# Output tiles at the seam of two attention stages, bias additions in other units, and the last two tiles stored apart

## The chip, the cores and the metric

The kernel runs on one core of a Trainium2 chip. Every time is a device time in microseconds (us) of one execution. Engines are named as the profile names them: PE is TensorE's matmuls and PEld its weight loads, DVE is VectorE, ACT is ScalarE, POOL is GpSimd, SP is SyncE, which here only issues DMAs.

## The reference, cut to what matters

One transformer block on two batches of 1024 rows of 256 columns, all float32. `x_attn` attends to itself and then to a context of 154 rows of 192; both have 16 heads of 64.

```
h = layernorm(x, ln1_g, ln1_b)
x = attention(h, h, sa_wq, sa_wk, sa_wv) @ sa_wo + sa_bo + x
h = layernorm(x, ln2_g, ln2_b)
x = attention(h, cond, ca_wq, ca_wk, ca_wv) @ ca_wo + ca_bo + x
h = layernorm(x, ln3_g, ln3_b)
p = h @ ff_w1 + ff_b1                      # 2 x 1024 columns: a, gate
x = (a * gelu(gate)) @ ff_w2 + ff_b2 + x
```

A bias such as `sa_bo` is one row of 256 that is added to every row of x. It can be added to x at any time after layernorm has read x for this attention and before the next layernorm reads it.

## The kernel before, in words

x stays in SBUF, in tiles of 128 rows (`xt`). For each batch there are 8 of them. The whole program is written as one fixed order of slots: `tc.manual_schedule()` means that each engine gets its instructions in the order in which the Python code issues them. Each engine works through its own queue in that order and waits on semaphores where data or a buffer isn't ready.

**Self attention, 128 slots `p` (16 units of 8).** A unit is a batch and a pair of heads; units 0 to 7 are batch 0, units 8 to 15 batch 1. In one slot, PE computes two groups of 64 query rows' scores (`s`, L381, eight matmuls each; the profile counts each float32 matmul as two). DVE takes their row maxima (`st`, L541). ACT takes the exponentials (`p`, L392), with the sums beside. Halves of the rows' statistics lie on other partitions, so SP exchanges them with four small DMAs (`st<-st`, L402). One slot later POOL joins them (`dd` L410 to L412, then `ee` on ACT L414, then `zz`, `den` L416 and L418), DVE takes reciprocals (`rd`, L488), and POOL scales the exponentials (`p`, L492). Two slots later DVE transposes them (`pT`, L506). The other half of a slot's PE time is either a quarter of a head pair's weighted values (`po`, L428), in four slots out of eight, or pieces from lists: `run_work` takes from `work` (projections of the next unit: `pq`, `pk`, `pv`), from `side` (pieces of a layernorm) and from `outs` (output tiles). Without `full`, a slot takes one such piece, with it two:

```
full = hg % 2 == 0 or outs or p >= SA - 2 * SH
run_work(2 if full else 1, 1, sum_tile)
```

The score tiles come from a PSUM pool of two, so the scores of a slot wait until the exponentials of the slot before are taken. Projections and output tiles share another PSUM pool of two (`mm`), which is freed by ACT's copies or DVE's additions.

**Output tiles (`out_piece`, L354).** Four matmuls (`py`) multiply half of the heads' results for 128 rows with `wo`, and DVE adds the result to x in the next slot (L366). Batch 1's first half of heads is complete after unit 11. Its 8 tiles are `("sa", 1, 0, t)`: tiles 0 to 3 go into units 12 and 13, two a unit, tiles 4 to 7 into unit 15.

**Bias additions (`add_biases`, L255).** They put one addition for each of the 8 tiles on `later`. A self attention slot takes one function from `later`, a context attention slot up to two. The addition is POOL's (L261). For batch 0's self attention they are queued before the first slot, behind weight loads; for others `norm_beside` queues them at the end of the layernorm's pieces. After the last addition of batch 1, the next stage's bias is loaded by SP into the same tile.

**Context attention, 48 slots `c`, three a unit,** and then the feed forward, 64 slots `k`. Slot `c` = 0 follows slot `p` = 127 directly; the last slots' transposes, joins and weighted values of self attention run out beside the slots `c` = 0 to 4 (`self_drain`, `self_values`). The scores there are `sc` (L653), their maxima `neg` (L658), and the projections `pq_ca`, `pk_ca`, `pv_ca`. The place where self attention ends and context attention begins is called the seam. The feed forward ends with `sum_slot`, whose `store` (L847) adds two tiles' sums to x and stores both with one DMA.

Of the kernel before, what the change touches and what calls it, by code (L numbers as in the profile page):

```python
# [10 lines left out]
ALU = mybir.AluOpType  # L11
AX = mybir.AxisListType

P = 128
# [4 lines left out]
def tile_transformer_block(ctx: ExitStack, tc: tile.TileContext, a: dict, out: bass.AP):  # L19
    nc = tc.nc  # L20
# [10 lines left out]
    NT = S // P  # L31
# [235 lines left out]
    def norm_beside(kind, b):  # L267

        after = {"sa": None, "ca": "sa", "ff": "ca"}[kind]
        stats, deviation, normalize, turn = norm_pieces(kind, b)
        n = 1 if narrow(kind, b) else 2
        lag = {}
        for fns, first in ((turn, 3), (stats, 0), (deviation, 1), (normalize, 2)):
            for i, fn in enumerate(fns):
                t = i if fns is stats else 2 * i + 1
                lag.setdefault(first + t // n, []).append((fn, fns is turn))
        for k in range(NT // n + 3):  # L280
            tiles = range(k * n, min((k + 1) * n, NT))
            needs = [(after, b, half, t) for half in range(2) for t in tiles if after]

            def step(fns=lag[k]):
                done = [fn() for fn, _ in fns]
                return next((fn for fn in done if fn), None)

            side.append((any(turns for _, turns in lag[k]), needs, step))
        side.append((False, (), lambda: add_biases(kind, b)))


    def project_half(dst, name, wt, h, n, mul=None, parts=1):
# [261 lines left out]
    def self_beside(ui):  # L554

        if ui + 2 >= NU:
            load_pair("ca", ui + 2 - NU)
        elif ui > 0:
            load_pair("sa", units[ui + 2][1])
        nxt = self_pieces(*units[ui + 1]) if ui + 1 < NU else cross_pieces(*units[0])  # L560
        if ui + 1 < NU:
            work.extend(nxt)
        else:

            spare["out"] = mm_tile
            last = [lambda t=t: out_piece("sa", B - 1, 0, t) for t in range(NT // 2, NT)]
            work.extend(nxt[:2] + last[:2])
            held.extend(nxt[2:] + last[2:])
        if HP <= ui < NU - 2:
            ob, oh = divmod((ui - HP) // HP, 2)  # L570
            t0 = (ui % HP) * 2
            out_pieces("sa", ob, oh, (t0, t0 + 1))
        if ui == 1:
            norm_beside("sa", 1)
        if ui == NPAIR + HP:
            norm_beside("ca", 0)

# [254 lines left out]
    def sum_slot():  # L832

        k = gated.pop(0)
        blk, f = divmod(k, NF)
        b, t0 = divmod(blk * TF, NT)
        if f == 0:
            sums[blk] = [sum_tile(f"pf{blk}_{i}") for i in range(TF)]
        for i in range(TF):
            nc.tensor.matmul(  # L840
                sums[blk][i][:, :D], lhsT=sums[blk, "u"][:, f, i * P:(i + 1) * P], rhs=w2[:, f, :],
                start=(f == 0), stop=(f == NF - 1),
            )
        if f < NF - 1:
            return None

        def store():  # L847
            for i in range(TF):
                t = t0 + i
                xs = xt[b, t // GT][:, t % GT, :]  # L850
                nc.vector.tensor_tensor(xs, sums[blk][i][:, :D], xs, ALU.add)
            t = t0 % GT
            nc.sync.dma_start(
                out=out[b, t0 * P:(t0 + TF) * P, :].rearrange("(t p) d -> p t d", p=P),
                in_=xt[b, t0 // GT][:, t:t + TF, :],
            )

        return store


    with tc.manual_schedule():
        stats, deviation, normalize, turn = norm_pieces("sa", 0, True)
        q0, q1, k0, k1, *values = self_pieces(*units[0])
        spare["bank"] = sum_tile

        def emit(*pieces):
            for piece in pieces:
                run(piece)
            flush(stores)


        warm = mm_tile("warm")

        def busy(n):
            for _ in range(n):
                nc.tensor.transpose(warm[:, :P], ident, ident)

        busy(32)
        emit(stats[0], stats[1], deviation[0])
        emit(stats[2], normalize[0], stats[3], deviation[1])  # L880
        copies = turn[0]()
        busy(10)
        emit(stats[4], normalize[1])
        copies()
        emit(stats[5], deviation[2])
        copies = turn[1]()
        busy(4)
        copies()
        emit(normalize[2], stats[6], stats[7], deviation[3])
        q_copy, copies = q0(), turn[2]()  # L890
        emit(normalize[3])
        q_copy()
        copies()
        k_copy, copies = k0(), turn[3]()
        k_copy()
        copies()
        emit(k1)
        later.append(lambda: load_pair("sa", units[1][1]))
        later.append(lambda: load_pair("sa", units[2][1]))
        later.extend(lambda t=t: load_x(nc.scalar, B - 1, t) for t in range(0, NT, 2))  # L900
        later.append(lambda: load_out("sa", nc.scalar))
        side.append((True, (), turn_rows))
        side.extend((True, (), lambda b=b: turn_context(b)) for b in range(B))
        work.extend([q1] + values)
        add_biases("sa", 0)

        for p in range(SA):
            if p % (2 * SH) == 0:
                self_beside(p // (2 * SH))
            if p == SA - SH:  # L910
                work.extend(held)
                held.clear()
            then = self_first(p)
            flush(stores)
            late = then()
            if p >= LAG:
                turn_groups(p - LAG)
            flush(adds)
            if late:
                late()  # L920
            if later:
                later.pop(0)()
            h, hg = divmod(p, SH)
            if h == 0 or hg < LAG:

                full = hg % 2 == 0 or outs or p >= SA - 2 * SH
                run_work(2 if full else 1, 1, sum_tile)
            else:
                run(lambda: self_values(h - 1, hg - LAG))

        for c in range(CA):
            if c == 0:
                pTc["ring"] = pt_.tile(
                    [P, 2 * NK, QH // 2], F32, tag="pT", name="pT_ca"
                ).rearrange("p a b -> p (a b)")[:, :3 * 2 * NB * NT * KB].rearrange(
                    "p (u n j q) -> p u n j q", u=3, n=NB, j=2)
            if c == SH + 1:
                out_pieces("sa", B - 1, 1, range(NT))
                outs.append(lambda: load_out("ca"))
            if c == SH + 1:  # L940
                w1, w2 = hold_gated()
            if c % len(CG) == 0:
                cross_beside(c // len(CG))
            if c % len(CG) == len(CG) - 1:
                work.extend(held)
                held.clear()
            flush(adds)
            then = cross_first(c)
            flush(stores)
            flush(lates)  # L950
            lates.append(then())
            if c <= SH:
                self_drain(SA + c)
            cross_regroup(c)
            cross_drain(c)
            cross_weigh(c)
            flush(stores)
            run_work(2, 1, n_sum=2 * (SH < c < 2 * NPAIR and c % len(CG) == 0))
            if SH - LAG < c <= SH:
                run(lambda: self_values(2 * NU - 1, c - SH + LAG - 1))  # L960
            for _ in range(min(2, len(later))):
                later.pop(0)()

        for k in range(FF):
            c = CA + k
            flush(adds)
            gate_slot(k)
            flush(stores)
            flush(lates)
            if k == 3 * len(CG):  # L970
                norm_beside("ff", B - 1)
            cross_regroup(c)
            cross_drain(c)
            cross_weigh(c)
            flush(stores)
            if k == 0:
                out_pieces("ca", B - 1, 0, range(NT - 2 * TF, NT))
            if k == len(CG) + 2:
                out_pieces("ca", B - 1, 1, range(NT))
            if k > len(CG) + 2:  # L980
                for _ in range(min(2, len(gated) - 1)):
                    run(sum_slot)
                flush(stores)
            run_work(2, 1)
            if later:
                later.pop(0)()
        while gated:
            run(sum_slot)
            flush(stores)
# [32 lines left out]
```

## Time and profile before

| | us |
|---|---|
| runs of the kernel before, three | 1166.22, 1167.21, 1169.26; median 1167.21 |
| profiled execution | 1166.33 |
| its span, first to last instruction | 1164.5 |
| PE busy in the span | 1141.3 (98%) |
| DVE, ACT, POOL busy | 828.9, 643.3, 665.8 |
| POOL bias addition, one (L261) | 0.73 |
| DVE addition of an output tile (L366) | 0.41 |
| matmuls of one output tile, eight records in the trace | 1.8 |
| mean granted TensorE clock | 0.997 |

A clock of 1 is TensorE's full speed. A line of the profile names the line of the kernel (L261), the tile that is written and the tiles that are read (`x<-x,sa_bo`), and, in brackets, how long the engine had been idle and what released it.

### The profile page before, as it was taken

To read this page: it belongs to the slowest core of one execution; us is meant where nothing else is said; L and a number is where in the kernel's file an instruction comes from. 1 tells how busy PE (TensorE), PEld (TensorE's weight loads), DVE (VectorE), ACT (ScalarE), POOL (GpSimd) and SP (SyncE) were. 2 spreads that over 40 slices of the span, in tenths; PEclk is the share of its full clock that TensorE was granted. 3 is DMA by queue.
4 is the path that set the end of the run, shared out by engine and by line. 5 is a ranking of instruction groups with operands and counts; after the bars stand their busy time and mean duration, and the time that the engine had idled before them with its cause. 6 is when DMAs were issued, how large, how long until landed. Compare 5 with 4: busy or idle time off the path is not lost.

```text
span 1164.5 us, 31710 instructions
## 1 busy us (share of the span) xinstructions
PE 1141.3 (98%) x11931; PEld 673.2 (58%) x11931; DVE 828.9 (71%) x1170; ACT 643.3 (55%) x2055; POOL 665.8 (57%) x1556
## 2 busy tenths in 40 slices
PE   8999999999999999999999999899999999999998
PEld 5434444545545545545545455565566567888887
DVE  4888998898889889888999899557555664232222
ACT  5666676666666656656666666538655572041111
POOL 1778777876777777677777788626644453030000
PEclk9999999999999999999999999899999999999999
DMA  2311011111101101101111010167444433000000
GB/s 80 98 41 34 12 26 34 21 21 34 21 16 35 21 17 26 26 19 21 25 26 21 18 29 11 42 159 183 115 104 99 99 82 69 7 13 10 19 10 18
DMA packets 87234, 51.21 MB, mean 44 GB/s; under 512 B 30814, under 2 KB 77866, under 8 KB 87082
## 3 DMA queue, kind: packets, MB, share of 16 engines
q1 hardware_dynamic: 83866, 46.57, 17.5%
q10 hardware_dynamic: 3216, 2.62, 0.7%
q8 instruction: 94, 1.54, 0.6%
q14 instruction: 58, 0.48, 0.1%
HBM read 19.52 MB, written 2.10 MB: 19 GB/s over the span
## 4 chain that ended last, share of the span: by engine, by line
PE 82%; ACT 6%; POOL 3%; DVE 3%; DMA 2%; issue 2%; SPq 1%; DVEq 0%; ACTq 0%; POOLq 0%
PE po L428 16%; PE s L381 16%; PE pa L817 10%; PE py_sa L359 5%; PE py_ca L359 5%; PE pq_ca L298 5%; PE pf L840 5%; PE poc L729 4%; ACT p L392 4%; PE pv_sa L314 4%; PE pk_sa L298 3%; PE sc L653 3%; PE pq_sa L298 3%; DMA st<-st 2%; DVE st L541 2%
## 5 line engine op out<-in xcount | busy, mean ns | idle before, releaser
L392 ACT ACTIVATE p<-s,st 128x512 f32<-128x512 f32 x512 | 344.7, 685 | 217.9 <-DVE st L541 206.3
L492 POOL TENSOR_SCALAR p<-p,rd,ee 128x512 f32<-128x512 f32 x512 | 385.6, 767 | 43.7 <-DVE rd L488 42.7
L541 DVE TENSOR_REDUCE st<-s 128x2 f32<-128x1024 f32 x256 | 301.2, 1218 | 43.1 <-PE s L381 34.7
L506 DVE STREAM_TRANSPOSE pT<-p 128x1024 f32<-128x1024 f32 x256 | 302.3, 1218 | 1.7 <-POOL p L492 1.7
L381 PE MATMUL s<-k_sa,q_sa 64*32 64x512 f32 x4096 | 253.4, 596 | 12.5 <-ACT p L392 11.2
L428 PE MATMUL po<-pT,v_sa 64*64 64x256 f32 x4096 | 235.8, 379 | 0.0
L428 PEld LDWEIGHTS po<-pT,v_sa 64*64 64x64 f32 x4096 | 150.4, 133 | 109.1 <-issue 37.0
L680 POOL TENSOR_SCALAR p<-p,rden 128x154 f32<-128x154 f32 x256 | 96.8, 398 | 118.3 <-DVE rden L677 118.1
L669 ACT ACTIVATE p<-sc,neg 128x154 f32<-128x154 f32 x256 | 95.8, 394 | 86.6 <-DVE rden L677 82.9
L381 PEld LDWEIGHTS s<-k_sa,q_sa 64*32 64x32 f32 x4096 | 60.0, 105 | 142.4 <-issue 54.5
L817 PE MATMUL pa<-hT_ln,wf 128*128 128x256 f32 x512 | 121.0, 379 | 0.0
L826 DVE SCALAR_TENSOR_TENSOR u<-pa,cols,gate 128x256 f32<-128x256 f32 x64 | 30.9, 484 | 124.2 <-ACT gate L823 124.2
L823 ACT ACTIVATE gate<-pa,cols 128x256 f32<-128x256 f32 x64 | 30.3, 473 | 152.2 <-PE pa L817 152.2
L817 PEld LDWEIGHTS pa<-hT_ln,wf 128*128 128x128 f32 x512 | 96.8, 190 | 13.7 <-issue 0.8
L392 ACT ACTIVATION_READ_ACCUMULATOR p<-s,st 128x1 f32 x512 | 103.7, 202 | 0.0
L658 DVE TENSOR_REDUCE neg<-sc 128x6 f32<-128x924 f32 (+1 forms) x48 | 48.4, 1009 | 51.1 <-PE sc L653 51.1
L416 POOL TENSOR_TENSOR zz<-ee,st 128x8 f32<-128x8 f32 x128 | 25.9, 202 | 76.8 <-ACT ee L414 76.8
L314 PEld LDWEIGHTS pv_sa<-sa_wv,hT_ln 128*128 128x128 f32 x512 | 59.3, 192 | 16.3 <-issue 13.8
L840 PE MATMUL pf<-wf,u 128*128 128x256 f32 x256 | 65.0, 379 | 0.2 <-DVE u L826 0.2
L298 PE MATMUL pq_ca<-hT_ln,ca_wq 128*128 128x512 f32 x128 | 61.9, 625 | 0.5 <-ACT hT_ln L240 0.5
L314 PE MATMUL pv_sa<-sa_wv,hT_ln 128*128 128x128 f32 x512 | 62.4, 278 | 0.0
L359 PE MATMUL py_ca<-ca_wo,o_ca 128*128 128x256 f32 x256 | 60.8, 384 | 0.3 <-ACT hT_ln L240 0.3
(73 smaller groups left out, 1229.4 us busy)
## 6 DMA issues: line engine op xcount, KB each, us to landing
wf<-pT_ca SPq DMA_DIRECT2D x128, 128.0 KB, 2.4
st<-st SPq DMA_DIRECT2D x512, 1.0 KB, 1.7
v_sa<-v_sa SPq DMA_DIRECT2D x64, 128.0 KB, 2.5
wf<-in_L_xattn_ff_w_dram SPq DMA_DIRECT2D x12, 256.0 KB, 5.8
sa_wq<-in_L_xattn_sa_wq_dram SPq DMA_DIRECT2D x16, 128.0 KB, 2.3
sa_wk<-in_L_xattn_sa_wk_dram SPq DMA_DIRECT2D x16, 128.0 KB, 2.4
sa_wv<-in_L_xattn_sa_wv_dram SPq DMA_DIRECT2D x16, 128.0 KB, 2.4
ca_wq<-in_L_xattn_ca_wq_dram SPq DMA_DIRECT2D x16, 128.0 KB, 2.5
```

The source lines that it names most:

```text
L298: nc.tensor.matmul(pq[:, own], lhsT=wt[:, c, :], rhs=h[:, c, n * HB + own.start:n * HB + own.stop], start=(c == 0), stop=(c == NC - 1),)
L314: nc.tensor.matmul(pv[:, i * P:(i + 1) * P], lhsT=h[:, c, (n * GT + i) * P:(n * GT + i + 1) * P], rhs=wt[:, c, :], start=(c == 0), stop=(c ...
L359: nc.tensor.matmul(py[:, :D], lhsT=o[:, i, t * P:(t + 1) * P], rhs=wo[kind][:, half * HP + i, :], start=(i == 0), stop=(i == HP - 1),)
L381: nc.tensor.matmul(sc[a4 * KB:(a4 + 1) * KB, j, :], lhsT=q[r, c:c + KB], rhs=k[r, h * HB:(h + 1) * HB], start=True, stop=True, tile_positi ...
L392: nc.scalar.activation(pr[:, j, :], sc[:, j, :], AF.Exp, bias=st[:, 0, 0, i, j:j + 1], accum_out=st[:, 0, 1, i, j:j + 1],)
L428: nc.tensor.matmul(po[a2][j * DH:(j + 1) * DH, :QH // 2], lhsT=v[r, t, e, j * DH:(j + 1) * DH], rhs=pT[r, j * NK + n, :], start=(t == 0 an ...
L492: nc.gpsimd.tensor_scalar(pr[:, j, :], pr[:, j, :], rd[:, c:c + 1], ee[:, 0, c:c + 1], op0=ALU.mult, op1=ALU.mult,)
L506: nc.vector.transpose(halves[h][:, :, c:c + KB], groups.pop(0).rearrange("p j (n k) -> p (j n) k", k=KB))
L541: nc.vector.tensor_reduce(st[:, 0, 0, i, :], sc[i], AX.X, ALU.max, negate=True)
L680: nc.gpsimd.tensor_scalar(pr_[:, j, i, :T], pr_[:, j, i, :T], rden[:, j, i:i + 1], 1.0, op0=ALU.mult, op1=ALU.mult,)
L817: nc.tensor.matmul(pa[:, half, :TF * P], lhsT=w1[:, c, half * DF + f * P:half * DF + (f + 1) * P], rhs=h[:, c, t0 * P:(t0 + TF) * P], star ...
L840: nc.tensor.matmul(sums[blk][i][:, :D], lhsT=sums[blk, "u"][:, f, i * P:(i + 1) * P], rhs=w2[:, f, :], start=(f == 0), stop=(f == NF - 1),)
```

## The change

The kernel's instructions are the same, but for one DMA more. They stand in another order:

- `norm_beside` no longer queues the bias additions of self attention (either batch) or of context attention's batch 0. Self attention's are queued at the start of unit 4 (batch 0) and unit 6 (batch 1), so each unit's eight slots take one each. Before, batch 0's ran through unit 1 and batch 1's through unit 4. The load of `ca_bo`, which follows batch 1's, moves to unit 7. Context attention's batch 0 additions are queued at its slot 5, behind the feed forward's weight loads; before, they ran in unit 15.
- Output tiles 4 and 5 of batch 1's first half go from unit 15 into unit 14 (counted from 0; the fifteenth unit), where `outs` then makes `full` true for two slots, so that half a key projection and half a value projection come one to four slots earlier. Tiles 6 and 7 go behind the slots `c` = 1 and 2.
- In unit 15 a slot takes one piece instead of two.
- The last two tiles are stored by two DMAs of 128 KB, the first from SP right after the first addition, the second from ACT.

```
-        side.append((False, (), lambda: add_biases(kind, b)))
+        if not narrow(kind, b):
+            side.append((False, (), lambda: add_biases(kind, b)))
...
-            spare["out"] = mm_tile
-            last = [lambda t=t: out_piece("sa", B - 1, 0, t) for t in range(NT // 2, NT)]
-            work.extend(nxt[:2] + last[:2])
-            held.extend(nxt[2:] + last[2:])
-        if HP <= ui < NU - 2:
+            work.extend(nxt[:2])
+            held.extend(nxt[2:])
+        if HP <= ui < NU - 1:
             ob, oh = divmod((ui - HP) // HP, 2)
             t0 = (ui % HP) * 2
             out_pieces("sa", ob, oh, (t0, t0 + 1))
         if ui == 1:
             norm_beside("sa", 1)
+        if ui in (HP, HP + 2):
+            add_biases("sa", (ui - HP) // 2)
...
-            for i in range(TF):
+            n = TF if blk < B * NBL - 1 else 1
+            for i in range(0, TF, n):
+                for t in range(t0 + i, t0 + i + n):
+                    xs = xt[b, t // GT][:, t % GT, :]
+                    nc.vector.tensor_tensor(xs, sums[blk][t - t0][:, :D], xs, ALU.add)
                 t = t0 + i
-                xs = xt[b, t // GT][:, t % GT, :]
-                nc.vector.tensor_tensor(xs, sums[blk][i][:, :D], xs, ALU.add)
-            t = t0 % GT
-            nc.sync.dma_start(
-                out=out[b, t0 * P:(t0 + TF) * P, :].rearrange("(t p) d -> p t d", p=P),
-                in_=xt[b, t0 // GT][:, t:t + TF, :],
-            )
+                (nc.scalar if i else nc.sync).dma_start(
+                    out=out[b, t * P:(t + n) * P, :].rearrange("(t p) d -> p t d", p=P),
+                    in_=xt[b, t // GT][:, t % GT:t % GT + n, :],
+                )
...
-        add_biases("sa", 0)
...
-                full = hg % 2 == 0 or outs or p >= SA - 2 * SH
+                full = (hg % 2 == 0 or outs) and p < SA - 2 * SH
...
+            if c == 1:
+                out_pieces("sa", B - 1, 0, range(NT - 2, NT))
             if c == SH + 1:
                 out_pieces("sa", B - 1, 1, range(NT))
                 outs.append(lambda: load_out("ca"))
             if c == SH + 1:
                 w1, w2 = hold_gated()
+                add_biases("ca", 0)
```

`narrow(kind, b)` is true for self attention and for context attention's batch 0. HP is 4, SH is 4, NU is 16, NT is 8, SA is 128, TF is 2.

## The prediction

> **What bounds the kernel now.** I read the page first, then the windows of its stages, then, where TensorE (PE) idles, its timeline and the chain of waits. The page says that PE is nearly the whole span:
>
> ```profile
> PE 1141.3 (98%) x11931; PEld 673.2 (58%) x11931; DVE 828.9 (71%) x1170; ACT 643.3 (55%) x2055; POOL 665.8 (57%) x1556
> ```
>
> The edits issue the same matmuls in another order, so they can gain only where PE stands idle or runs at a low clock, and at the tail. The windows show where that is. Columns: stretch, length, PE, PEld, DVE, ACT, POOL busy, granted clock, DMA share, GB/s.
>
> ```profile
> 60.60:107.60 47.00, 42.02 (x568) 19.33 (x564) 40.79 (x50) 28.60 (x85) 38.31 (x82) 1.00 0.11 22
> 107.60:153.60 46.00, 42.80 (x575) 20.31 (x571) 40.99 (x51) 31.25 (x91) 34.23 (x79) 1.00 0.11 23
> 153.60:196.50 42.90, 42.18 (x573) 20.55 (x570) 38.58 (x42) 30.00 (x89) 33.21 (x74) 1.00 0.12 25
> ...
> 682.70:725.70 43.00, 43.00 (x568) 22.00 (x564) 38.89 (x45) 26.52 (x81) 35.91 (x78) 1.00 0.06 12
> 725.70:743.90 18.20, 14.91 (x70) 7.98 (x66) 12.65 (x18) 11.58 (x54) 14.59 (x38) 0.81 0.14 40
> 736.20:743.90 7.70, 7.66 (x22) 3.77 (x22) 4.93 (x9) 4.41 (x21) 5.73 (x18) 0.59 0.00 1
> ```
>
> These are units 1, 2, 3 and 15 and the seam (context attention's slots 0 to 3). Unit 1 loses 5 us of PE time, unit 15 nothing, the seam over 3 us idle, and then it runs 7.7 us at clock 0.59. The chain of waits inside unit 1 passes through the bias additions:
>
> ```profile
> 88.76 0.73 POOL x L261
> 89.89 0.26 POOL dd L412
> 90.17 0.22 ACT ee L414
> 90.46 0.21 POOL zz L416
> 91.26 3.01 POOL p L492 x4
> 94.27 0.70 POOL x L261
> ```
>
> They take 5.7% of the 50 us from 60 to 110, 2.86 us. The order is bias addition, then the next slot's `dd`, `ee`, `zz`, then the scaling: POOL is a closed round. PE's timeline at the seam:
>
> ```profile
> 730.38 1.06 PE L653 MATMUL sc<-k_ca,q_ca 64*128 64x154 f32 x12
> 732.40 0.79 PE L605 MATMUL pk_ca<-ctxT,ca_wk 96*128 96x154 f32 x4 [0.97 <-ACT q_ca L307]
> 733.12 0.79 PE L653 MATMUL sc<-k_ca,q_ca 64*128 64x154 f32 x8
> 736.24 1.91 PE L653 MATMUL sc<-k_ca,q_ca 64*128 64x154 f32 x12 [2.32 <-ACT k_ca L609]
> 738.08 5.88 PE L298 MATMUL pq_ca<-hT_ln,ca_wq 128*128 128x512 f32 x8
> 743.89 1.31 PE L428 MATMUL po<-pT,v_sa 64*64 64x256 f32 x20
> ```
>
> Two idles, 0.97 and 2.32, and then the same shapes cost 1.91 and 5.88 instead of 1.06 and 3.70 (the row of the same kind at 726.75): 3.0 us lost to the clock. The seam loses 6.3 us in all.
>
> [...]clock 0.59 follows two idles that sum to 3.3 us; [...]and the 1.8 us one before 72.51 left the clock at 1.00. [...]here the `k_ca` copy that PE awaits at 736.24 starts at 735.87, right after six exponentials. [...]the output stores here land in 2.1 us for 256 KB.
>
> **The change part by part.** *Bias additions of sa, batch 0: unit 1 to unit 4.* Eight of 0.73 us, 0.66 of it net in POOL's round. With one, rounds of `rd` last 5.48 (80.02 to 85.50); without, POOL alone needs 4.80 (722.40 to 727.20), and DVE, its reductions, transposes and reciprocal back to back, 5.01 (149.59 to 154.60), 0.54 more with a batch-norm tile. So DVE is late next. Followed through unit 1: `rd` at 68.95 comes 0.42 earlier (now held by ACT's exponentials, which end at 67.70). The next two rounds are DVE's and keep that. The rounds of 5.48 that end at 85.50 and 90.98 become about 5.3 (the exchange, below) and 5.0 (DVE): 1.0 ahead. The one to 97.55 loses its 0.66: 1.8 ahead. The last two wait on the exponentials (0.87) and on the exchange DMA (0.64), so they keep 1.8 and give no more. Unit 2 starts 1.8 earlier; all its waits follow `rd`, so it hands this on. Bounds: 0 (other waits take over) to 2.86 (the chain's share). I take **-1.8**.
>
> *Their new place, units 4 and 6.* There PE needs 1.88 + 3.62 = 5.50 us a slot and POOL with an addition 5.47. Unit 4 carries additions now (batch 1's) and takes 44.0 for eight slots, all PE; unit 6 has the same work. Cover: PE; without it 0.66 a slot. **0**. The `ca_bo` load moves 16 slots down SP's queue, one issue between two exchanges as before: 0.
>
> *Unit 14.* The second half of `pk_sa` and output tiles 4, 5 come in: slots 113 and 117 grow from 3.7 to 5.5 us. They were slack (0.5 us of stalls), so unit 15 starts at 684.9 instead of 682.74.
>
> *Unit 15.* Its slots 120, 121, 124, 125 drop from 5.5, 5.5, 4.5, 5.5 us of PE work to 3.7, 3.7, 2.5, 3.8. Others now set the pace, by rules read from this trace: a reduction starts 1.25 after its scores start, no sooner than 5.01 after the last (0.64 more with two output tiles added) nor 10.1 to 10.6 after the one two slots back (668.51 to 678.60; 652.06 to 662.62: the exchange DMA); scores start 2.76 after the last reduction starts, their second half 4.10 after. Slot starts become 684.9, 688.9, 693.9, 700.0, 705.5, 709.7, 714.9, 720.8, and context slot 0 726.2, against 725.76: +0.4. The late start is nearly paid back; PE idles some 5.5 us there in pieces of 0.3 to 2. The ca additions have left, so POOL (4.80) stays below DVE.
>
> *The seam.* Tiles 6 and 7 are still to do, 1.83 us each. `pk_ca` waits for the `q_ca` copy as before, but the addition at 730.17 (0.66) is gone ahead of `dd`, so about 732.4; tile 6 runs to 734.9, `sc` to 735.6. Tile 7 needs the PSUM bank that the `k_ca` copy frees at 736.0: 0.4 idle, then it runs to 737.9, `sc` to 738.9. The queries, at full clock, run to 742.5, against 743.89. DVE's two additions (0.35) come before two reductions that have slack. So **-1.3**: the bound runs from -3.0 (slot 0 starts on time) to +0.5 (exchange at its slow end), without the clock.
>
> *ca additions, eight, two a slot, during rstd near 800.* POOL's work in those slots grows from 4.0 to 5.4 in pieces; DVE and PE have their next need 2 to 3 us later (DVE idles 2.56 and 3.03 at 798.39 and 810.85). **+0.1**, between 0 and 0.6.
>
> *Tail.*
>
> ```profile
> 1160.57 0.85 DVE L851 TENSOR_TENSOR x<-pf,x 128x256 f32<-128x256 f32 x2 [0.86 <-PE pf L840]
> 1161.45 0.37 SPq L853 DMA_DIRECT2D out_dram<-x  x1
> ```
>
> The second tile's store still starts at 1161.4, now from ACT's idle queue, with 128 KB instead of 256: [...]ACT's issue isn't shown for stores, so from -0.4 to +0.3. **-0.2**.
>
> Sum: -1.8 + 0 - 1.3 + 0.1 - 0.2 = -3.2. The profiled execution took 1166.33 (span 1164.5 and 1.8 around it): 1163.1. The runs' median, 1167.21, stands 0.9 above it: **1164.0**.
>
> **The rivals.** *A, more:* the chain's whole 2.86 goes in unit 1, and unit 15's idle is absorbed so that the seam gives its -3.0: -2.9 - 3.0 - 0.1 = -6, 1161.2. For it: 2.86 lies on the chain. Against: DVE's 5.01 stands right behind. *B, the additions were hidden anyway:* unit 2 holds none and still takes 46.0, so the exchange and DVE set unit 1 too: -0.2 there, -1.6 in all, 1165.6. Against: rounds of exactly 5.48. *C, slower:* unit 15 starves PE. If its eight slots take unit 2's 5.75 (46.0) instead of the 41.3 that I worked out, +4.7, and the gap of up to 2.1 us before slot 125's scores lets the clock fall for one stretch like that at 736 (+3.0): -3.2 + 7.7 = +4.5, 1171.7. It decides from 5.56 us a slot (3.2/8 over 5.16) without the clock. For it: two waits of unlike kind (DMA, DVE) meet there. Against: unit 2's batch-norm and square roots aren't in unit 15. *D:* the order doesn't change. Excluded: the two instruction orders differ as described.
>
> **How the numbers follow.** Forecast 0.52 (own range 1162.7 to 1165.7), A 0.17, B 0.16, C 0.15. A measurement can tell about 0.3%, 3.5 us, from no change. Faster by more: all of A and 0.23 of the forecast's 0.52, 0.40. Slower by more: most of C, 0.12. Same: 0.48. The range 1160.4 to 1169.0 takes in A and the lower part of C.
>
> **What would show it.** Right: rounds near 5.0 to 5.4 in unit 1, and unit 2 starting about 1.8 sooner; units 4 and 6 at 44.0; context slot 0 within 1 us of 725.8 less that 1.8, PE idle inside unit 15; no clock under 0.9 at the seam. Wrong: the clock falling in unit 15, a unit 1 of 47 us, or a unit 6 above 44.5.

## The result, and the profile after

| | before | changed |
|---|---|---|
| median of 11 runs each, side by side | 1166.68 (1165.81 to 1169.28) | 1164.57 (1163.48 to 1167.95) |
| span of the profiled execution | 1164.5 | 1162.8 |

The ratio is 0.998, with a 95% interval from 0.9971 to 0.999: the change gains about 2 us, less than the 3.5 us that I had named as what a measurement can tell. The forecast was 1164.0. The granted clock isn't the same in the eleven executions of the changed kernel: its mean is 0.999 or 1.000 in eight, and 0.995 to 0.997 in the three slowest (1165.78, 1167.06, 1167.95). The profiled execution is one of the eight.

Total busy time on the page of the changed kernel; PE's busy share is still 98%:

```profile
PE 1139.2 (98%) x11931; PEld 672.2 (58%) x11931; DVE 829.5 (71%) x1170; ACT 644.5 (55%) x2055; POOL 669.2 (58%) x1556
```

The number of matmuls is the same, and PE is busy 2.1 us less. At the seam alone, the scores and queries that ran at half clock before cost 3.0 us less (timeline below). The windows of the changed kernel, for units 1, 2, 14, 15 and the seam from context slot 0 to the first `po` of slot 3 (columns as in the prediction):

```profile
60.85:106.85 46.00, 41.99 (x564) 19.31 (x560) 40.77 (x50) 28.39 (x85) 32.98 (x74) 1.00 0.11 23
106.85:152.55 45.70, 42.81 (x572) 20.32 (x568) 40.99 (x51) 31.28 (x91) 34.54 (x79) 1.00 0.11 23
...
638.41:683.44 45.03, 45.03 (x588) 23.67 (x585) 39.23 (x44) 30.36 (x89) 33.07 (x75) 1.00 0.12 24
683.44:724.57 41.13, 37.30 (x536) 15.78 (x532) 38.38 (x41) 26.60 (x82) 32.06 (x72) 1.00 0.06 11
724.57:742.09 17.52, 15.46 (x84) 9.31 (x81) 12.82 (x20) 10.36 (x50) 13.80 (x35) 1.00 0.16 45
```

Unit 1 is 1 us shorter, with POOL busy 33.0 instead of 38.3. Unit 14 has no idle PE left and takes 45.03. Unit 15 has PE idle for 3.8 of 41.13 us, and the clock holds. The seam takes 17.52, at a clock of 1.00. Units 4 and 6, which now hold self attention's additions, take 44.16 each, as units 4 to 12 did before.

In unit 1, the chain of waits of the changed kernel, which passed through `x` at L261 twice, now runs so (shorter pieces left out):

```profile
87.46 1.74 DMA st<-st
89.81 0.26 POOL dd L413
90.09 0.22 ACT ee L415
90.38 0.21 POOL zz L417
91.18 3.03 POOL p L493 x4
```

No addition is on it. But the statistics exchange is: the DMA comes ahead of `dd` in the place where I expected only DVE and POOL.

PE's timeline at the seam of the changed kernel:

```profile
731.71 0.79 PE L606 MATMUL pk_ca<-ctxT,ca_wk 96*128 96x154 f32 x4 [1.46 <-ACT q_ca L308]
732.33 1.89 PE L360 MATMUL py_sa<-sa_wo,o_sa 128*128 128x256 f32 x8
...
735.55 1.99 PE L360 MATMUL py_sa<-sa_wo,o_sa 128*128 128x256 f32 x8 [0.60 <-ACT k_ca L610]
737.47 1.06 PE L654 MATMUL sc<-k_ca,q_ca 64*128 64x154 f32 x12
738.46 3.70 PE L299 MATMUL pq_ca<-hT_ln,ca_wq 128*128 128x512 f32 x8
742.09 3.68 PE L429 MATMUL po<-pT,v_sa 64*64 64x256 f32 x64
```

The two output tiles stand there, and the same scores and queries that had cost 1.91 and 5.88 now cost 1.06 and 3.70: in this execution the clock doesn't fall. But the wait ahead of `pk_ca` has grown from 0.97 to 1.46, and tile 7 waits for the `k_ca` copy with the scores of slot 3 behind it. The source of the longer wait is on POOL's timeline, same kernel:

```profile
730.23 0.20 POOL L411 TENSOR_TENSOR dd<-st 128x4 f32<-128x4 f32 x1 [1.67 <-DMA st<-st]
```

The tail, on the timeline of the changed kernel:

```profile
1159.58 0.35 SPq L855 DMA_DIRECT2D out_dram<-x  x1
1160.01 0.36 ACTq L855 DMA_DIRECT2D out_dram<-x  x1
```

From the last store's issue to the end of the span it takes 2.8 us, and took 3.1 before. The same 2.8 stands in all eight profiled executions with two stores, and the 3.1 in all five with one.

Where the profiled 1.7 us come from, by the starts of slots: unit 2 starts 0.73 earlier than before, unit 4 1.02, context slot 0 1.19, `po` of slot 3 1.80. Then 0.34 is given back at context slot 14, where `poc` waits 0.22 and 0.57 for a DMA (800.27 and 801.49); the tail adds 0.3.

### The profile page after: what moved, and what is told of

Same layout as the page of the kernel before. It is cut to its first block, busy times and chain, and to the rows that moved or that the text cites. A ratio compares the mean times of both kernels' runs of the same rounds, so it can differ in the third digit from the quotient of the medians.

```text
span 1162.8 us, 31708 instructions
## 1 busy us (share of the span) xinstructions
PE 1139.2 (98%) x11931; PEld 672.2 (58%) x11931; DVE 829.5 (71%) x1170; ACT 644.5 (55%) x2055; POOL 669.2 (58%) x1556
## 3 DMA queue, kind: packets, MB, share of 16 engines
q8 instruction: 94, 1.54, 0.5%
## 4 chain that ended last, share of the span: by engine, by line
PE 79%; ACT 8%; DVE 4%; POOL 3%; DMA 3%; issue 2%; SPq 1%; DVEq 0%; ACTq 0%; POOLq 0%
PE po L429 15%; PE s L382 15%; PE pa L818 10%; ACT p L393 6%; PE py_ca L360 5%; PE pf L841 5%; PE py_sa L360 5%; PE pq_ca L299 4%; PE poc L730 4%; PE pk_sa L299 4%; PE pq_sa L299 4%; PE pv_sa L315 3%; PE sc L654 3%; DVE st L542 2%; DMA st<-st 2%
## 5 line engine op out<-in xcount | busy, mean ns | idle before, releaser
L299 PE MATMUL pk_sa<-hT_ln,sa_wk 128*128 128x512 f32 (+1 forms) x132 | 60.6, 596 | 0.3 <-ACT q_sa L308 0.3
```

Source lines behind the costliest of these rows:

```text
L299: nc.tensor.matmul(pq[:, own], lhsT=wt[:, c, :], rhs=h[:, c, n * HB + own.start:n * HB + own.stop], start=(c == 0), stop=(c == NC - 1),)
```

## The experiments

Three theories stood at the start. **The additions:** the gain is the bias additions' leaving POOL's round in unit 1. **The tiles:** it is the seam. **Together:** the tiles only pay if context attention's additions leave unit 15, because those keep POOL at 5.48 us a slot there. All medians are to be read against the kernel before, run on the same chip; intervals are 95%.

**Self attention's additions alone.** The kernel before, with these only:

```
+        if kind != "sa":
             side.append((False, (), lambda: add_biases(kind, b)))
+        if ui in (HP, HP + 2):
+            add_biases("sa", (ui - HP) // 2)
-        add_biases("sa", 0)
```

> The kernel before with one part of the change: self attention's bias additions in units 4 and 6 instead of units 1 and 4. Theory (POOL's closed round sets unit 1): unit 1 shrinks from 47.0 to about 46.0 and unit 2 from 46.0 to 45.7, units 4 and 6 stay at 44.16, everything behind moves 1.3 us forward: ratio 0.9989. Rival (the additions were hidden, and the whole gain of the change comes from the seam): units 1 and 2 unchanged, ratio 1.000.

Measured: 1164.81, ratio 0.9981 (0.9973 to 0.9989), span 1162.4. That is as much as the whole change. In its profiled execution the 2.16 us of its slots come from three places: 1.12 up to unit 15, -0.32 in slot 125, and 1.36 at the seam, where I had expected nothing. There the same idles stand as before (0.99 and 2.32), and still the low clock costs only 1.6 instead of 3.0 (the queries take 5.05, 1.35 more than at full speed, the scores 1.35, 0.29 more). The stretches at half clock, in the windows of the kernel before and of this one:

```profile
735.67:742.50 6.83, 6.26 (x17) 3.38 (x18) 5.34 (x9) 4.58 (x24) 6.26 (x20) 0.50 0.00 1
```

```profile
736.09:739.50 3.41, 3.41 (x12) 1.55 (x9) 3.41 (x8) 1.84 (x9) 3.41 (x12) 0.50 0.01 2
```

The low clock lasted 6.83 us in the one and 3.41 in the other. In the kernel before, PE came back from its idle at 736.24, 0.57 behind the fall at 735.67, and in this one at 735.46, 0.63 ahead of the fall at 736.09. The idles are as long in both, so they alone don't tell what the low clock costs; what sets its start and its length, these runs don't show. The prediction had taken the loss of one execution, 3.0, for a constant.

The 1.36 belongs to this one execution, not to the median. Nine of this kernel's 13 executions show the mean clock that the profile of before shows, 0.997. Their median is 1164.86, against 1166.83 for the 23 of before with 0.997 that ran beside them. At the same clock the additions are thus worth 2.0 us, which is about the whole gain.

**The tiles alone.** The kernel before with `last` removed from unit 15, `HP <= ui < NU - 1`, the new `full`, and tiles 6 and 7 at `c == 1`; every addition as before:

> The kernel before with the output tiles and the single pieces of unit 15 as in the changed kernel, all bias additions and the last store as before. Theory: with the additions of context attention's batch 0 still in unit 15, POOL's round of 5.47 takes PE's place there, so unit 15 lasts about 43.3 instead of 41.1; unit 14 costs its 2.1; the clock stays up at the seam; in all 1.5 to 2.5 us slower than before, ratio 1.0013 to 1.0021. Rival (the tiles alone make the seam's gain): unit 15 lasts 41 to 41.5 and the kernel is 0.4 to 0.8 us faster, ratio 0.9995.

Measured: 1167.83, ratio 1.0009 (1.0001 to 1.0017), span 1165.9. The tiles alone cost about 1 us.

**Context attention's batch 0 additions alone,** moved to slot 5:

```
-        side.append((False, (), lambda: add_biases(kind, b)))
+        if kind != "ca" or not narrow(kind, b):
+            side.append((False, (), lambda: add_biases(kind, b)))
...
                 w1, w2 = hold_gated()
+                add_biases("ca", 0)
```

> The kernel before with only context attention's batch 0 additions moved to the slots from c = 5. Theory: unit 15 is bound by PE at 43.0 with or without them, and at the seam the statistics' exchange arrives no earlier, so between 0 and -0.5 us there, and 0 to +0.4 beside the rstd near 800: ratio 0.9998 to 1.0002, and the clock still falls. Rival (the additions held up the seam): 1 to 3 us faster, the idle ahead of the fourth sc under 1.5 us, and the clock stays up.

Measured: 1165.15, ratio 0.9986 (0.9979 to 0.9993), span 1162.2. My theory said no change. The rival was right in the time, but not in its signs: the idle stays, and the clock falls. PE's timeline at the seam of this kernel:

```profile
731.48 0.79 PE L606 MATMUL pk_ca<-ctxT,ca_wk 96*128 96x154 f32 x4
...
735.31 1.91 PE L654 MATMUL sc<-k_ca,q_ca 64*128 64x154 f32 x12 [2.32 <-ACT k_ca L610]
737.15 4.49 PE L299 MATMUL pq_ca<-hT_ln,ca_wq 128*128 128x512 f32 x8
```

Unit 15 and slots 0 and 1 stand where they did (725.70 against 725.76). The last addition, which stood ahead of the last `dd` on POOL, is gone, and with it the wait ahead of `pk_ca`: slot 2 starts 0.92 earlier. The idle is 2.32 as before, and the clock falls: 1.6 lost instead of 3.0. That 1.4 is again this execution's: 4 of the kernel's 22 executions have a mean clock of 1.000, so that it fell in none of their stages, and 10 have 0.997 or less. After slot 4 the gain of 2.32 stands to the last context slot, so the additions' new place, two a slot near 800, costs nothing.

**Tiles and context attention's additions together,** self attention's additions and the tail as before:

> The kernel before with tiles and context attention's additions as in the changed kernel, without self attention's additions moved and with the last store as before. Theory (the parts of head, seam and tail add up): unit 14 +2.1, unit 15 -1.9, seam -0.6, 0.4 us faster than before, ratio 0.9996; with self attention's -1.3 and the tail's -0.3 that makes the 2.1 of the whole change. Rival (the seam brings most): ratio 0.9985 or less.

Measured: 1166.95, ratio 1.0004 (0.9994 to 1.0013), span 1164.6. So adding the tiles to the context additions costs 1.8 us (1165.15 to 1166.95), and adding them to nothing costs 1.1 (1166.70 to 1167.83): they lose both ways. The windows of unit 15, first of the tiles alone, then with the additions gone from it:

```profile
685.08:727.90 42.82, 38.42 (x536) 15.75 (x532) 37.50 (x40) 26.36 (x80) 36.42 (x79) 0.96 0.05 11
```

```profile
685.33:726.37 41.04, 37.31 (x537) 15.80 (x533) 38.39 (x41) 26.51 (x82) 31.85 (x72) 1.00 0.06 11
```

The work of PE is the same. With the additions POOL is busy 36.4 instead of 31.9, the unit takes 42.8 instead of 41.0, and what unit 14 took (2.1) isn't paid back. The clock even falls once there (0.96): PE idles for 2.29 us ahead of the scores of slot 125, which then take 3.31 us instead of 1.95. That is what rival C foresaw. But the clock fell there without the additions too, in the profiled execution of the version with the tiles in other banks (below), where the unit took 41.77. Read from one execution each, some 0.7 of the 1.8 goes with the fall, and 1.1 is left to the additions. So "together" holds for unit 15: without its additions, it pays back. It doesn't hold for the whole, because the seam takes the gain: from slot 0 to `po` it takes 17.6 us here, and 15.9 with the context additions alone.

**All additions and the tail, no tile.** The changed kernel with the tile edits undone:

> The kernel before with all bias additions moved (self attention's to units 4 and 6, context attention's batch 0 to its slot 5) and the last two tiles stored one by one; the output tiles stay in unit 15, and `full` is as before. THEORY (the parts add up where no tile moves: the additions leave POOL's round in unit 1 and stand no longer ahead of dd at the seam): unit 1 and 2 give 1.0 as in e1, the 0.97 us wait ahead of pk_ca goes as in e3 (-0.9), the 2.32 us wait ahead of the scores of context slot 3 stays and so does one stretch of low clock (1.6 us lost instead of 3.0, -1.4), the tail gives 0.26: -3.6 in all, 1163.1 us, ratio 0.9969, below the changed kernel's 1164.57. RIVAL (e1 and e3 gained the same 1.4 us of clock each, by chance of where the stretch fell): -1.0 -0.9 -0.3 = -2.2, 1164.5, ratio 0.998, no better than the changed kernel.

Measured: 1162.74, ratio 0.9973 (0.9963 to 0.9984), span 1161.2. It is 1.8 below the changed kernel, though the intervals of the two ratios overlap (those of the context additions with and without the tiles, above, don't). The parts add up as the theory had it, and the low clock again costs 1.6. From slot 0 to `po` it takes 16.1 us, the changed kernel 17.52. These 1.4 are: `dd` 1.1 later behind slot 0 (5.66 against 4.58 us), the scores of slot 3 1.9 later behind `dd` (7.24 against 5.33), and 1.6 less for scores and queries at full clock. Two things were therefore to be explained: the 1.9, and the 1.1.

**The 1.9: tile 7's PSUM bank.** Each tile at the seam is put one place earlier, in a bank of the weighted values:

```
-            if c == 1:
-                out_pieces("sa", B - 1, 0, range(NT - 2, NT))
...
+            if c in (1, 2):
+                spare["out"] = sum_tile
+                run(lambda: out_piece("sa", B - 1, 0, NT - 3 + c))
             run_work(2, 1, n_sum=...)
```

> The changed kernel with output tiles 6 and 7 computed in the PSUM banks of the weighted values instead of the shared pool of two, and each one place earlier on PE: tile 6 ahead of pk_ca in context slot 1, tile 7 ahead of the scores of slot 2. THEORY (tile 7 waits for the bank that ACT's k_ca copy frees, and so stands behind that copy with its whole 1.9 us, instead of in the idle time ahead of it): tile 6 fills the 1.46 us wait for q_ca, tile 7 the wait for k_ca, the scores of slot 3 start right after the k_ca copy, near 735.6 instead of 737.47, and the end comes 1.9 earlier: 1162.7 us. RIVAL (DVE's two additions then come ahead of the reciprocal and the reduction that ACT's exponentials need, and the k_ca copy comes later by as much): within 0.5 us of the changed kernel, 1164.6.

Measured: 1162.95, ratio 0.9975 (0.9964 to 0.9985), span 1160.5. PE's timeline at its seam:

```profile
732.31 0.69 PE L606 MATMUL pk_ca<-ctxT,ca_wk 96*128 96x154 f32 x4
...
733.66 1.99 PE L360 MATMUL py_sa<-sa_wo,o_sa 128*128 128x256 f32 x8
735.58 1.06 PE L654 MATMUL sc<-k_ca,q_ca 64*128 64x154 f32 x12
```

No wait is left in front of any of them. From slot 0 to `po` it takes 15.3 us, 2.2 less than in the changed kernel, and the median is 1.6 lower. The cause is shown: tile 7 had waited for the bank that the `k_ca` copy frees (0.60 in the changed kernel, nothing here), and the scores of slot 3, which waited for the same copy and stand behind it in PE's order, came behind its whole 1.9 us (735.55, then 737.47). The tile had been put behind the wait that it was to fill. Bank and place were changed together; what either does alone isn't shown. In unit 15, whose instructions are those of the changed kernel, the clock fell in this execution, from 709.54 to 712.95.

**The 1.1: first theory.** In the changed kernel SP issues three `v_ca` copies right behind the exchange of slot 127. Here they come later (`later` isn't taken from in slot 127 and in context slots 0 and 1):

> The changed kernel with one thing moved: SP's last three v_ca copies are issued at context slot 2, behind three weight loads, instead of right behind the statistics exchange of slot 127. THEORY (the three v_ca DMAs share the queues with that exchange and hold it up, so dd waits 1.67 us there): dd waits under 0.5, pk_ca's wait for q_ca falls from 1.46 to about 0.3, tile 7 and everything after it stand 1.2 us earlier: 1163.4 us against 1164.6. RIVAL (the exchange of slot 127 is late for another cause, its own four issues after a late reduction): dd still waits 1.6, 1164.6 us.

Measured: 1164.7, ratio 0.9986 (0.998 to 0.9993). `dd` still waits 1.39. The copies aren't the cause, and the theory fell.

**The 1.1: second theory.** The exchange's transfers themselves are on the DMA engines from 725.7 to 727.7, and `dd` starts at 730.23. What lies there besides, the copies apart, is one packet of another queue. From the DMA view of the changed kernel, for 727.5 to 728.0 (queue and kind: packets, MB, share of 16 engines):

```profile
q8 instruction: 1, 0.02, 15.2%
```

There are 94 such packets in the kernel, 16 KB each (1.54 MB). The profile names their kind, `instruction`, but no engine. That they bring TensorE's instructions is my estimate, from its 23862 matmuls and weight loads, some 254 a packet; the expectations below call them its fetches. I then counted, from 60 to 740 us in six profiled executions (before, changed, two versions with one tile moved, two with a longer head), the exchanges whose `dd` waited for the DMA. With such a packet 1.75 to 4.25 us ahead of `dd`, 188 of 251 waited. Without, 31 of 482 did. The other seven profiled executions give 202 of 290 and 39 of 564. To move the packets against the work, 26 matmuls without a use were added at the head, as here, and in another kernel 52 (20 wide ones and 64 narrow ones):

```
-        busy(32)
+        busy(26)
+        for _ in range(32):
+            nc.tensor.transpose(warm[:, :16], ident[:16, :], ident[:16, :16])
```

> The changed kernel with 26 matmuls more at its head (6 of the 32 warm-up transposes replaced by 32 narrow ones of 16 columns; no result depends on them), so that everything after stands 26 matmuls and as many weight loads later in TensorE's instruction stream. THEORY (at the seam of the changed kernel a 16 KB fetch of TensorE's instructions, seen on the DMA engines at 727.7, falls into the exchange of slot 127, and dd starts 2.5 us behind it instead of 1.3 behind the last issue; moved 52 instructions, the fetch falls near 724, ahead of the exchange's transfers): dd waits under 0.5 instead of 1.67, and context slot 0 to the weighted values takes 16.4 us instead of 17.52. The head may cost up to 0.5 and other exchanges be hit or spared, so the whole is 1163.5 within 1.5. RIVAL (dd waits for the exchange's own four transfers, or for work on the cores that the fetch only accompanies): dd waits 1.4 to 1.7 again, 17.5 us, wherever the fetch falls.

> As e11_fetch32 with 52 matmuls more at the head (12 transposes replaced by 64 narrow ones). THEORY (the fetch): it falls near 722.5 at the seam, between two exchanges, and dd waits under 0.5 there; the waits of dd inside units 1 to 15 again follow the fetches, of which some two thirds of those 1.75 to 4.25 us ahead of a dd come with a wait, against 1 in 16 of the others. RIVAL (chance, or the order of the work): the waits stay at the slots where the changed kernel has them, slot 127 among them, whatever the fetches do.

Measured with 26: 1165.43, ratio 0.9985 (0.9978 to 0.9991). That is above the range expected, 1162.0 to 1165.0: the head costs 2.4 us, not 0.5 (the first scores `s` start at 20.28 instead of 17.84). The packet came at 726.9, not at 724; the exchange's four issues, which start there, took 3.03 us instead of the 2.44 of the changed kernel, and `dd` of slot 127 waits 0.40. But the packet before it now falls, at 718.5, 2.5 us ahead of `dd` of slot 126, and this one waits 1.38. The round of slot 127 starts that much later, and the seam takes 17.4, not the 16.4 expected. Measured with 52: the packet at 726.7 comes 5.7 us ahead of `dd`, which doesn't wait at all. PE's timeline at that seam:

```profile
732.78 1.06 PE L654 MATMUL sc<-k_ca,q_ca 64*128 64x154 f32 x12
733.80 0.79 PE L606 MATMUL pk_ca<-ctxT,ca_wk 96*128 96x154 f32 x4
```

The wait ahead of `pk_ca` is gone, and from slot 0 to `po` it takes 16.03 us instead of 17.52. The kernel as a whole is slower, 1168.77, ratio 1.0013 (1.0006 to 1.002): the head costs 4.9 us, not the 0.5 that I had set for it. The 64 narrow ones take 5.07 us, and the clock falls under them. From the windows of this kernel, 8 to 11 us:

```profile
8.00:11.00 3.00, 3.00 (x32) 2.96 (x32) 0.26 (x2) 1.10 (x2) 0.33 (x1) 0.58 0.39 122
```

PE shows as busy throughout, and the clock is 0.58. In each of the two kernels, 34 of the `dd` with a packet in the stretch named wait (of 40 and 42), and 6 without (of 82 and 81). Against the start of slot 0 the packet came 3.2 behind in the changed kernel, 1.1 behind with 26, and 1.5 ahead with 52: it moves with the number of TensorE's instructions ahead of it, as the estimate asks. The waits go with the packets; in what way a packet delays an exchange, no run shows.

**A version that beats both.** All additions and the tail as in the change; of the tiles only the seventh moves, into the 2.32 us idle and out of the pool of two:

```
-            last = [... for t in range(NT // 2, NT)]
+            last = [... for t in range(NT // 2, NT - 1)]
...
+            if c == 2:
+                spare["out"] = sum_tile
+                run(lambda: out_piece("sa", B - 1, 0, NT - 1))
```

> e9_adds_tail with one tile moved: tile 7 leaves unit 15 (slot 125) and stands ahead of the scores of context slot 2, in a PSUM bank of the weighted values; tiles 4, 5 and 6 stay in unit 15. THEORY (unit 15 has room for one tile less before DVE and the exchange set its pace, about 5.14 us a slot as in the changed kernel, and the 2.32 us idle at the seam takes one tile for nothing): 0.5 to 1.2 in unit 15, and the clock stays at 1.00, another 1.6: 2.1 to 2.8 below e9, 1160.7 us if e9 is 1163.1. RIVAL (slot 125 gives nothing, because DVE's reductions already stand 5.0 apart there and the two-slot exchange 10.6): only the clock's 1.6, 1.6 below e9. RIVAL 2 (the clock falls all the same[...]): 0.5 to 1.2 below e9.

Measured: 1161.84, ratio 0.996 (0.9948 to 0.9973), span 1159.1, 2.1 less span than without the tile. PE's timeline at the seam:

```profile
730.89 1.89 PE L360 MATMUL py_sa<-sa_wo,o_sa 128*128 128x256 f32 x8
732.71 0.79 PE L656 MATMUL sc<-k_ca,q_ca 64*128 64x154 f32 x8
734.10 1.06 PE L656 MATMUL sc<-k_ca,q_ca 64*128 64x154 f32 x12 [0.59 <-ACT k_ca L612]
```

The tile has filled the idle but for 0.59, and the clock holds (1.06 again): 1.6. Unit 15 gives 0.5, the lower end of what was expected: 1.0 in slot 125, and half of it is lost again in slot 126. By the medians the two differ by 0.9, within their intervals, so the 2.1 is the profile's figure. Against the changed kernel the gain is clear: the slowest of its five executions took 1162.63, the fastest of the changed kernel's eleven 1163.48. The same kernel with 26 matmuls more at the head:

> e10_one_tile with the 26 matmuls more at its head of e11_fetch32. There a fetch lies at 725.0, 3.8 us ahead of dd[...]. THEORY (the fetch): moved 52 instructions earlier it leaves that exchange, the 0.52 us wait ahead of pk_ca goes, and the seam is up to 0.5 shorter; over the whole kernel the hits even out, so within 1 us of e10's 1161.84. RIVAL (fetches cost nothing): the 0.52 stays.

Measured: 1161.63, ratio 0.995 (0.9937 to 0.9964). `dd` of slot 127 no longer waits, nor does `pk_ca`, and from slot 0 to `po` it takes 14.18 us instead of 14.64, the 0.5 expected.

## Why the prediction was right, and where not

The predicted time, 1164.0, is 0.6 below the measured median, inside the forecast's own range. Part of that nearness is luck: the gain was forecast as 3.2 and measured as 2.1, and the forecast started from a median of 1167.21, where the kernel before took 1166.68 beside the change. Step by step:

- **Additions out of unit 1, -1.8:** right in mechanism, and in size on average. In the profiled pair, unit 1's start to unit 4's takes 134.6 instead of 135.9, 1.3 less. Over all profiled executions it takes 134.2 on average in the nine with self attention's additions moved (133.9 to 134.6), and 136.2 in the four without (135.9 to 136.8), 1.9 to 2.0 less. The round from 85.32 to 90.90 was 5.58, where I had 5.0: it holds the exchange shown in the chain, with a packet of instructions ahead of it. One execution says this term to about half a us, no better; the additions moved alone gave 2.0 at the same clock.
- **Units 4 and 6, 0:** right. They are PE's, 44.16 each.
- **Unit 14, +2.2; unit 15, 41.3:** measured +2.1 and 41.13. The rules read from the trace of before, DVE's 5.01 and the exchange over two slots, held: with the unit's start 1.46 earlier than forecast, every slot of it starts within 0.4 of where it was put. Rival C's starved PE came (3.8 us idle), but cost nothing more in this execution. Whether the clock holds there differed between two executions of these instructions, as the last section shows. That the ca additions had to leave for this, the prediction said in half a sentence; the tiles alone showed that it is worth about 1.1, and 1.8 with the clock's fall. One reading was off, without consequence: the idle ahead of 72.51 is 1.62 in the trace, not 1.8.
- **The seam, -1.3:** the figure is made of +0.4 for units 14 and 15 together and of -1.8 from context slot 0 to `po` (16.3 instead of 18.1). Measured were +0.2 and -0.6, so the seam gave a third of what was put down for it. The term that failed is the start of `dd`. I let it follow POOL's scaling directly once the addition was gone, so `pk_ca` should start 6.2 us behind slot 0 (732.4 against 726.2). But `dd` waited 1.67 for the exchange, and `pk_ca` starts 7.1 behind slot 0: 0.9 of the 1.2 missing. With the packet elsewhere the seam took 16.03, against the 16.3 of the prediction (726.2 to 742.5). The tile behind the `k_ca` copy was in the sum, as 0.4 idle and 1.83; it came as 0.60 and 1.9. That the queries run at full clock was my estimate; they did in this execution (3.70).
- **What the seam's gain was put down to:** here the reasoning was wrong where the sum came out near. I counted the clock's 3.0 as the tiles' gain. But the loss was nothing in the profiled execution of the changed kernel, 1.6 with either set of additions moved alone and 3.0 before, the leaving of one addition ahead of `dd` gives 0.9 alone, and the tiles as the change places them cost 1.8 over the additions without them. I never priced the additions without the tiles.
- **ca additions near 800, +0.1; tail, -0.2:** 0 and -0.3. The tail's -0.2 was my estimate. The 0.34 given back at context slot 14 isn't theirs: it is missing in the kernel with these additions moved alone. Why `poc` waited there was not tried.

Rival B, additions hidden anyway, is refuted by self attention's additions moved alone. Rival A's 2.86 and 3.0 were not reached; its level, though not by its ways, is that of the version with one tile (1161.84).

## What to carry to other kernels

Work that is to fill an idle on an engine that runs in order must be able to start before the event that ends the idle: look not only where the gap is, but which buffer the filler takes, and what frees it. Tile 7, put behind the wait that it was to fill, cost the scores behind it 1.9 us. Price each part of a change alone and in pairs; the sum here came near while one of its parts, the largest edit, cost 1.8 us. And before one assigns tenths of a us from one pair of profiles, one should see how far the same stretch differs between executions that don't touch it.

## What the runs showed of the hardware

- Packets of 16 KB and of the kind `instruction` go over the DMA engines, 94 in the changed kernel; that they are TensorE's, one in some 254 of its matmuls and weight loads, is my estimate. Of the exchanges with such a packet 1.75 to 4.25 us ahead of `dd`, 75% waited (188 of 251; 1.67 us at the seam of the changed kernel), and 6% of the others (31 of 482). With 26 matmuls more at the head the wait of `dd` in slot 127 went from 1.67 to 0.40, and 1.38 came up in slot 126; with 52 more, `dd` of slot 127 didn't wait.
- Half clock lasted 6.83 us at the seam of the kernel before and 3.41 with self attention's additions alone, both with an idle of 2.32 us on PE. In the first the clock fell 1.75 us into that idle (735.67, the idle from 733.92 to 736.24), in the second 0.63 behind its end. With the tiles alone, PE idled for 2.29 us in unit 15 and the scores behind it took 3.31 us instead of 1.95. No fall followed the idle of 1.62 ahead of 72.51 in the kernel before, nor those of 1.46 and 0.60 at the seam of the changed kernel. The same instructions can go either way: in unit 15 the changed kernel had PE idle for 3.8 of 41.13 us at a clock of 1.00, and the version with the tiles in other banks fell to half from 709.54 to 712.95. How much idle lowers the clock, and when, these runs don't settle.
- Narrow matmuls, back to back, didn't keep the clock up in two kernels, though PE shows as busy all the time. Under 64 transpositions of 16 by 16 (5.77 to 10.84 us) it fell at 8.50, for 6.83 us; right behind 32 of them (6.52 to 8.61) it fell at 8.70, for 3.41. Under the 32 transpositions of 128 by 128 that stand there in the changed kernel (1.91 to 7.87) it rose to full speed at 6.55 (22 matmuls in the 4.64 us before that, 15 in the 1.45 from there to 8.00) and didn't fall.
